# An attention layer on one core: GpSimd's scalings get fixed places, and the start makes half of the masks and heads

## The chip, the cores and the metric

The kernel runs on one NeuronCore of a Trainium2 chip. The metric is the time of one execution on the device in microseconds, in medians of several runs. The engines are named as in the profile: PE is TensorE (PEld its weight loads), DVE is VectorE, ACT is ScalarE, POOL is GpSimd and SP is SyncE, which here only issues transfers.

## The reference

The input x has 8 batches of 2048 rows and 256 channels, the adjacency matrix adj 2048 x 2048 integers, the same for all batches. With 8 heads of 32 channels the reference computes

```python
qkv = einsum('fnc,ck->fnk', x, w_qkv)            # q, k, v: (F, N, 8, 32)
scores = einsum('fnhd,fmhd->fhnm', q, k) / sqrt(32)
scores = where(adj > 0, scores, -1e9)
attn = softmax(scores, axis=-1)
t = einsum('fhnm,fmhd->fnhd', attn, v)           # back to (F, N, 256)
y = layernorm(x + t, ln1_g, ln1_b)
h = relu(y @ w1 + b1)
z = layernorm(y + h @ w2 + b2, ln2_g, ln2_b)
out = layernorm(x + z)
```

All of it is in float32.

## The kernel before

Only the path for these shapes (`fast_path`) runs. A batch is cut into 4 chunks of 512 query rows (`qc`), 2 groups of 4 heads (`g`) and 16 blocks of 128 key rows (`mb`, called a phase below). An item is one (batch, chunk, group, block). There are 8 x 4 x 2 x 16 = 1024 items, and the main loop takes one per step; 16 steps are a group, 128 steps a frame, which is one batch.

A step t does this: `exponentials(t+1)` on ACT (L237), `scores(t+2)` as 8 matmuls on PE (L230) with two additions of the mask on DVE (L233), `values(t)` as 8 matmuls on PE (L249), and `add_up(t)`. The last prepares the softmax denominators: blocks 3, 6, 8, 10, 12 and 14 are added on POOL to the tile of block 0 (L271), and blocks 4, 7, 11 and 5, 9, 13 are added by accumulating transfers, issued by POOL, to the tiles of blocks 1 and 2 (L268). Block 15 stays alone. `denominator` (L315) sums the four tiles that are left over the keys on PE. A tile of items, `p`, holds 1 MB; there are 12 of them in a ring, and each becomes free when the last reader of its old content is done: the sum or the transfer for most blocks, `denominator` for four.

Everything else is a filler. `advance(t)`, first in a step, resumes generators from a list sorted by due time. What PE does for a filler needs one PSUM bank, and credit (2200 a step, 1024 for a group of products) says how many are taken in a step, unless one is due. `yield 3` rests three steps, `yield BANK` asks for the bank. The fillers are `denominator`, `outcome` (the division by the denominators and the residual, fetched by an accumulating transfer), `tail`, and the next batch's rows (`turn`), projections (`project`) and queries (`ask`), which the table NEXT starts at fixed steps of a frame.

`tail` of a chunk is: `norm` (statistics on DVE L278 and L279, small operations on POOL, scaling on ACT L290), `feed_forward` with two products and on POOL a multiplication and an addition on 128 x 1024 (L459 and L461), a second `norm`, again a multiplication and an addition on POOL (L363 and L365), an accumulating transfer that adds x (L367), a third `norm`, and the output. On each engine, and on POOL's queue of transfers, instructions run in the order in which the program issues them.

`begin`, ahead of the loop, turns the rows of batch 0, projects both head groups, and makes the mask of all four chunks from adj: 16 loads of 1 MB, a conversion on DVE (L575), transposes on PE (L141), evacuation to fp8 on ACT (L147) or DVE (L145), and a store to a DRAM tensor MD. In the loop `load_mask` fetches each chunk's masks from MD.

Of the kernel before, what the change touches and what calls it, by code (L numbers as in the profile page):

```python
# [31 lines left out]

MASKED = -57344.0
CODE = -5.0
# [27 lines left out]
def fast_path(ctx, tc, cst, x, adj, out, RS):  # L62
# [7 lines left out]
    ld = ctx.enter_context(tc.tile_pool(name="ld", bufs=LD))  # L70
    kp = ctx.enter_context(tc.tile_pool(name="kp", bufs=3 * NCK - 1))
    qp = ctx.enter_context(tc.tile_pool(name="qp", bufs=4))
    vp = ctx.enter_context(tc.tile_pool(name="vp", bufs=3 * NCK - 1))
    pp = ctx.enter_context(tc.tile_pool(name="pp", bufs=12))
    work = ctx.enter_context(tc.tile_pool(name="work", bufs=1))
# [48 lines left out]
    MD = dp.tile([NCK, MB // 2, P, 2 * CH // 4], I32, name="md")  # L124
    MK = {}

# [6 lines left out]

    def mask_blocks(qc, mc, cv, to=None):
        for half in range(2):
            yield BANK
            ps = bank(BF16)
            for r in range(2):
                for j in range(TPC):
                    rr = 2 * half + r  # L140
                    nc.tensor.transpose(ps[:, r, j * P:(j + 1) * P], cv[:, j, rr * P:(rr + 1) * P], identb)  # L141
            k = 2 * mc + half
            m = to[half] if to else mask_piece(0, qc, k)
            if half:
                nc.vector.tensor_tensor(m, ps, cst["ones"][:, 0:1, None].to_broadcast([P, 2, CH]), ALU.min, saturate=False)  # L145
            else:
                nc.scalar.copy(m.bitcast(I8), ps)  # L147
            nc.sync.dma_start(MD[qc, k], words(m))

# [72 lines left out]
    def scores(item):  # L222
        f, qc, g, mb = item
        pt = PT[item] = pp.tile([P, 4, CH], F32, name="p")
        ps2 = [score_pair() for _ in range(2)]

        for half in (1, 0):
            for j in range(2):
                r = D * (2 * half + j)
                nc.tensor.matmul(ps2[half][:, j, :], KT[f, mb // TPC, g][r:r + D, (mb % TPC) * P:(mb % TPC + 1) * P],  # L230
                                 QT[f, qc, g][r:r + D, :], start=True, stop=True)
        for half, ps in enumerate(ps2):
            nc.vector.tensor_tensor(pt[:, 2 * half:2 * half + 2, :], ps,  # L233
                                    MK[f, qc, mb // 2][:, mb % 2, None, :].to_broadcast([P, 2, CH]), ALU.add)

# [36 lines left out]


    def norm(t, per=1):
        mv = small.tile([P, TPC, nc.vector.BN_AGGR_DIM], F32, name="mv")
# [11 lines left out]
        nc.gpsimd.tensor_scalar(nb, nb, -1.0, 1.0, op0=ALU.mult, op1=ALU.mult)  # L287
        yield 2
        for j in range(TPC):
# [7 lines left out]
    def denominator(f, qc, g, ready):  # L297
        grp = (f, qc, g)
        blocks = [ALONE, MOVED[0][0], POOLED[0], MOVED[1][0]]
        late = {2: ready - 1, 3: ready}  # L300
        if (f, qc, g) == items[-1][:3]:
# [31 lines left out]
    def outcome(f, qc):  # L333
        yield ROOM
        state["tails"] += 1
        xin = x[f, qc * CH:(qc + 1) * CH, :].rearrange("(p j) c -> p j c", p=P)
        y = yp.tile([P, TPC, C], F32, name="y")
        yield from divide(f, qc, y)
        nc.gpsimd.dma_start(y, xin, accum_op=ALU.add)
        begin = items.index((f, qc, 1, LAST)) + SUM + 2  # L340
        if (f, qc) == (F - 1, NCK - 2):
            start(begin + 5, tail(f, qc, y, xin, 2), begin + 8)
        else:
            start(begin + 10, tail(f, qc, y, xin), begin + 26)

# [10 lines left out]

    def tail(f, qc, y, xin, per=1):
        yield from norm(y, per)
        yield from feed_forward(y)
        yield 1  # L360
        z = y
        yield from norm(z, per)
        nc.gpsimd.tensor_tensor(z, z, rows(cst["g2r"]), ALU.mult)  # L363
        yield 1
        nc.gpsimd.tensor_tensor(z, z, rows(cst["be2r"]), ALU.add)  # L365
        yield 1
        nc.gpsimd.dma_start(z, xin, accum_op=ALU.add)  # L367
        yield 7
        yield from norm(z, per)
        nc.sync.dma_start(out[f, qc * CH:(qc + 1) * CH, :].rearrange("(p j) c -> p j c", p=P), z)  # L370
        state["tails"] -= 1
# [65 lines left out]
    def finish(f, qc):  # L437
        y = yp.tile([P, TPC, C], F32, name="y")
        xr, xb = state["rows"]
        yield from divide(f, qc, y)  # L440
        yT, hT = (work.tile([P, 2, CH], F32, name=n) for n in ("turned", "hT"))
        dst = out[f, qc * CH:(qc + 1) * CH, :].rearrange("(p j) c -> p j c", p=P)
        both = [half_rows(h, y, xr, xb, yT, hT, dst) for h in range(2)]
        while both:
            for e in list(both):
                if next(e, both) is both:
                    both.remove(e)

    def feed_forward(y):
        yield TURNED  # L450
        state["turned"] = True
        yT = work.tile([P, 2, CH], F32, name="turned")
        for a in range(2):
# [3 lines left out]
            nc.scalar.activation(yT[:, a, :], ps, AF.Identity, bias=cst["be1c"][:, a:a + 1], scale=cst["g1c"][:, a:a + 1])  # L457
        yield 1
        nc.gpsimd.tensor_tensor(y, y, rows(cst["g1r"]), ALU.mult)  # L459
        yield 1  # L460
        nc.gpsimd.tensor_tensor(y, y, rows(cst["be1b2r"]), ALU.add)  # L461
        hT = work.tile([P, 2, CH], F32, name="hT")
# [8 lines left out]
        state["turned"] = False  # L471
        yield 1
        z = y
# [62 lines left out]
    items = [(f, qc, g, mb) for f in range(F) for qc in range(NCK) for g in range(2) for mb in range(MB)]  # L536
    LEAD = 2
    FRAME = 2 * NCK * MB


    def ask(f, c):
# [4 lines left out]
    NEXT = {1: [(turn, 0)], 2: [(ask, 1)], 20: [(turn, 1)], 34: [(ask, 2)], 40: [(project, 0, 0)], 50: [(turn, 2)],  # L546
            60: [(project, 1, 0)], 66: [(ask, 3)], 72: [(turn, 3)], 80: [(project, 2, 0)], 98: [(ask, 0)], 100: [(project, 3, 0)],
            104: [(project, 0, 1)], 108: [(project, 1, 1)], 112: [(project, 2, 1)], 116: [(project, 3, 1)]}

    def begin():  # L550
        todo = deque((qc, c) for qc in range(NCK) for c in range(NCK))
        rows, cols = [], deque()

        def fetch():
            if todo:
                qc, c = todo.popleft()
                t = pp.tile([P, 4, CH], F32, name="p").bitcast(I32)
                nc.sync.dma_start(t, adj[qc * CH:(qc + 1) * CH, c * CH:(c + 1) * CH].rearrange("(j p) m -> p j m", p=P))
                cols.append((qc, c, t))

        for c in range(NCK):
            rows.append(pp.tile([P, 4, CH], F32, name="p"))
            xc = rows[c][:, 0:2, :].rearrange("p a (b c) -> p (a b) c", c=C)
            nc.sync.dma_start(xc, x[0, c * CH:(c + 1) * CH, :].rearrange("(j p) c -> p j c", p=P))
            fetch()
        fetch()
        while cols:
            qc, c, col = cols.popleft()
            if c % 2 == 0:
                two = pp.tile([P, 4, CH], F32, name="p").rearrange("p a q -> p (a q)").bitcast(BF16)  # L570
            cv = two[:, c % 2 * TPC * CH:(c % 2 + 1) * TPC * CH].rearrange("p (j m) -> p j m", m=CH)

            for half, what in enumerate((CODE, MASKED)):
                part = slice(half * 2 * P, (half + 1) * 2 * P)
                nc.vector.tensor_scalar(cv[:, :, part], col[:, :, part], 0.0, what, op0=ALU.is_le, op1=ALU.mult)  # L575
            fetch()
            xT = rows[c][:, 2:4, :]
            if qc == 0:
                yield from turn_rows(rows[c][:, 0:2, :].rearrange("p a (b c) -> p (a b) c", c=C), xT)
                nc.sync.dma_start(XD[0][c], xT)  # L580
                XT[0, c] = xT
                if c == 0:
                    yield from queries(0, 0, xT)
                yield from project(0, c, 0, xT)
            elif qc == 1:
                yield from project(0, c, 1, xT)
            if qc and c % 2 == 0:
                out4 = take([P, 4, 2, CH], F8)
                give(out4)
            yield from mask_blocks(qc, c, cv, [out4[:, c % 2 * 2 + i] for i in range(2)] if qc else None)  # L590
            if (qc, c) == (1, NCK - 1):
                for k in range(LEAD):
                    scores(items[k])
                exponentials(items[0])

    for _ in begin():
        pass
    state["side"] = 0
    for t, (f, qc, g, mb) in enumerate(items):
        if g == 1 and mb % 2 and (f + 1 < F or qc + 1 < NCK):  # L600
            load_mask(f + (qc + 1) // NCK, (qc + 1) % NCK, mb // 2)
        for what, *which in NEXT.get(t % FRAME, []):
# [268 lines left out]
```

## Time and profile before

| | us |
|---|---|
| median of the runs (3194.78 to 3200.07) | 3196.82 |
| the profiled execution | 3199.32 |
| its span | 3197.5 |
| first score matmul, PE L230 | 59.50 |
| first exponential of the loop (item 1) | 96.0 |
| starts of frames 1 to 7 | 466.7, 846.5, 1229.4, 1612.4, 1995.6, 2378.6, 2761.6 |
| last exponential | 3147.5 |

The span goes from the first to the last instruction of the profiled execution. A frame's start is the start of the exponential of its second item on ACT, the first that the frame's first step issues. The page gives for each group of instructions its busy time, the mean of one in ns, and the idle time of the engine ahead of it with what ended most of it. For a transfer it gives the time from issue to landing. Times in a timeline are from the start of the span.

### The profile page before, as it was taken

How to read it: one execution, taken by the hardware profiler on the slowest of the kernel's cores; microseconds unless marked ns; L12 is line 12 of the kernel's file. 1: busy time of each engine (PE TensorE's matmuls, PEld its weight loads, DVE VectorE, ACT ScalarE, POOL GpSimd, SP SyncE). 2: the span in 40 equal slices, each digit the busy share in tenths (PEclk: the TensorE clock that was granted, in tenths of full speed). 3: DMA queues.
4: the chain of work that ended last, by engine and by line, in shares of the span. 5: the costliest groups of instructions: out<-in, count | busy, mean ns of one | idle time of the engine just before them, and what ended most of it. 6: DMA issues, size and time to landing. Idle time of an engine off the chain costs nothing.

```text
span 3197.5 us, 68542 instructions
## 1 busy us (share of the span) xinstructions
PE 3098.8 (97%) x28996; PEld 980.3 (31%) x28996; DVE 2737.4 (86%) x3203; ACT 2438.4 (76%) x1941; POOL 2589.4 (81%) x1358
## 2 busy tenths in 40 slices
PE   7899999999999999999999999999999999999985
PEld 4222333233332333323333323323233233332222
DVE  4788888888889988888988988888888888889975
ACT  3677778778778777788777788778878778778764
POOL 0478888888888888789888889888888788879884
PEclk8899999999999999999999999999999999999998
DMA  9588889788879888789878889878889788878863
GB/s 322 141 193 189 181 180 194 178 190 193 182 175 210 186 191 175 175 193 208 190 172 176 190 185 221 174 169 199 180 193 207 170 191 196 178 170 167 178 142 71
DMA packets 153098, 589.49 MB, mean 184 GB/s; under 512 B 15024, under 2 KB 67760, under 8 KB 103888
## 3 DMA queue, kind: packets, MB, share of 16 engines
q0 software_dynamic: 64272, 433.75, 67.7%
q1 hardware_dynamic: 87696, 149.98, 13.4%
q8 instruction: 229, 3.75, 0.4%
q10 hardware_dynamic: 816, 1.31, 0.1%
q14 instruction: 85, 0.70, 0.1%
HBM read 146.67 MB, written 37.75 MB: 58 GB/s over the span
## 4 chain that ended last, share of the span: by engine, by line
PE 87%; DVE 5%; issue 2%; DMA 1%; POOL 1%; ACT 1%; DVEq 0%; ACTq 0%; POOLq 0%
PE s L230 32%; PE x L249 28%; PE x L54 16%; PE x L315 7%; DVE p L233 4%; PE x L95 4%; DMA p<-p 1%; DVE st L278 0%; POOL p L271 0%; DMA y<-in_x_dram 0%; DVE y L353 0%; ACT p L237 0%; PE s L54 0%; DVE mv L279 0%; ACT y L290 0%
## 5 line engine op out<-in xcount | busy, mean ns | idle before, releaser
L233 DVE TENSOR_TENSOR p<-s,mask 128x1024 f32<-128x1024 f32 x2048 | 2410.3, 1219 | 336.2 <-PE s L230 196.0
L237 ACT ACTIVATE p<-p 128x2048 f32<-128x2048 f32 x1024 | 1956.6, 1911 | 527.7 <-DVE p L233 453.7
L271 POOL TENSOR_TENSOR p<-p 128x2048 f32<-128x2048 f32 x382 | 1858.7, 4866 | 388.5 <-ACT p L237 388.2
L230 PE MATMUL s<-qT,kT 32*128 32x512 f32 x8192 | 1172.4, 642 | 40.9 <-DVE p L233 35.6
L249 PE MATMUL x<-p,v 128*32 128x512 f32 x8192 | 1092.7, 605 | 0.5 <-ACT oT L253 0.4
L230 PEld LDWEIGHTS s<-qT,kT 32*128 32x128 f32 x8192 | 320.8, 183 | 643.9 <-DVE p L233 602.5
L268 POOL DMA_DIRECT2D p<-p x382 | 408.1, 1070 | 78.4 <-ACT p L237 49.4
L249 PEld LDWEIGHTS x<-p,v 128*32 128x32 f32 x8192 | 161.4, 108 | 779.9 <-issue 289.8
L315 PE MATMUL x<-p,ones 128*32 128x512 f32 x2080 | 267.1, 592 | 0.6 <-DMA p<-p 0.5
L54 PE MATMUL x<-in,wqkv 128*32 128x512 f32 x1888 | 243.5, 592 | 0.0
L290 ACT ACTIVATE y<-y,nb,rs 128x256 f32<-128x256 f32 x372 | 218.4, 590 | 3.0 <-POOL nb L287 3.0
L278 DVE BATCH_NORM_STATS2 st<-y 128x6 f32<-128x256 f32 x372 | 155.1, 417 | 5.2 <-DMA y<-in_x_dram 5.2
L54 PE MATMUL x<-turned,w1s 128*32 128x512 f32 x992 | 122.5, 592 | 0.0
L54 PEld LDWEIGHTS x<-wqkv,in 128*32 128x32 f32 x3584 | 102.2, 110 | 63.5 <-issue 58.9
L54 PE MATMUL x<-w2s,hT 128*32 128x256 f32 x2016 | 121.1, 381 | 0.0
L54 PE MATMUL x<-wqkv,in 128*32 128x128 f32 x3584 | 117.3, 273 | 0.0
L315 PEld LDWEIGHTS x<-p,ones 128*32 128x32 f32 x2080 | 67.4, 110 | 156.8 <-issue 152.0
L54 PEld LDWEIGHTS x<-in,wqkv 128*32 128x32 f32 x1888 | 61.7, 110 | 140.9 <-issue 113.1
L284 POOL TENSOR_TENSOR rs<-rs,mhalf 128x4 f32<-128x4 f32 x93 | 96.2, 1035 | 7.7
L363 POOL TENSOR_TENSOR y<-y,g2r 128x1024 f32<-128x1024 f32 x31 | 99.3, 3205 | 1.9 <-ACT y L290 1.9
L365 POOL TENSOR_TENSOR y<-y,be2r 128x1024 f32<-128x1024 f32 x31 | 91.9, 2963 | 0.6
L54 PEld LDWEIGHTS x<-w2s,hT 128*32 128x32 f32 x2016 | 65.5, 111 | 70.5 <-issue 37.8
(116 smaller groups left out, 1342.1 us busy)
## 6 DMA issues: line engine op xcount, KB each, us to landing
p<-p POOLq DMA_DIRECT2D x382, 1024.0 KB, 9.7
in<-xd SPq DMA_DIRECT2D x87, 512.0 KB, 9.3
mask<-md SPq DMA_DIRECT2D x248, 128.0 KB, 7.9
y<-in_x_dram POOLq DMA_DIRECT2D x62, 512.0 KB, 9.5
p<-in_adj_dram SPq DMA_DIRECT2D x16, 1024.0 KB, 9.7
out_dram<-y SPq DMA_DIRECT2D x31, 512.0 KB, 5.9
in<-in_x_dram SPq DMA_DIRECT2D x29, 512.0 KB, 14.5
xd<-in SPq DMA_DIRECT2D x28, 512.0 KB, 10.7
```

Of the source, the lines that this page charges most:

```text
L54: nc.tensor.matmul(out[r:r + D], lhsT[:, r:r + D], rhs, start=start, stop=stop)
L95: nc.tensor.transpose(ps[:, j * P:(j + 1) * P], s, ident)
L230: nc.tensor.matmul(ps2[half][:, j, :], KT[f, mb // TPC, g][r:r + D, (mb % TPC) * P:(mb % TPC + 1) * P], QT[f, qc, g][r:r + D, :], start=Tr ...
L233: nc.vector.tensor_tensor(pt[:, 2 * half:2 * half + 2, :], ps, MK[f, qc, mb // 2][:, mb % 2, None, :].to_broadcast([P, 2, CH]), ALU.add)
L237: nc.scalar.activation(PT[item], PT[item], AF.Exp, scale=1.0 / math.sqrt(D))
L249: nc.tensor.matmul(O[grp][r:r + D, :], V[f, mb // TPC, g][:, mb % TPC, r:r + D], PT[item][:, h, :], start=(mb == 0), stop=(mb == LAST))
L268: nc.gpsimd.dma_start(PT[f, qc, g, chain[0]], PT.pop(item), accum_op=ALU.add)
L271: nc.gpsimd.tensor_tensor(first, first, PT.pop(item), ALU.add)
L278: nc.vector.bn_stats(st, t[:, j, :])
L290: nc.scalar.activation(t[:, j, :], t[:, j, :], AF.Identity, bias=nb[:, j:j + 1], scale=rs[:, j:j + 1])
L315: nc.tensor.matmul(ps[r:r + D, :], cst["ones"], term[:, h, :], start=(n == 0), stop=(n == len(blocks) - 1))
L363: nc.gpsimd.tensor_tensor(z, z, rows(cst["g2r"]), ALU.mult)
```

## The change

- `begin` makes the masks of chunks 0 and 1 only, from 8 loads, with all evacuations on ACT, and projects head group 0 only. `other_half` projects head group 1 of batch 0 as a filler in the first group.
- The masks of chunks 2 and 3 are made in the loop in 16 pieces, one `mask_job` begun every 5 steps from step 1. Each has one half of a tile of its own (`px`, which in later batches holds block 15).
- The ring of `p` tiles has 11 in place of 12, the pools of keys and values have one tile less.
- POOL's scaling operations wait for `calm()`: the phases 15, 0, 1, 2, 3, 4. The two closing ones (L363 and L365) are issued in one step. `tail` is split in `tail` and `closing`, with a due time of its own.
- `norm` rests `lag()` steps, from a table, where it rested 2. `denominator` reads its last block a step later.
- `load_mask` is issued 9 steps later; `project(2, 0)` and those after it move in NEXT.
- The last chunk but one starts its tail 3 steps later and adds preloaded rows on POOL in place of the accumulating transfer. `finish` gives the fillers a step in between.

```diff
-    kp = ctx.enter_context(tc.tile_pool(name="kp", bufs=3 * NCK - 1))
+    kp = ctx.enter_context(tc.tile_pool(name="kp", bufs=3 * NCK - 2))
...
-    pp = ctx.enter_context(tc.tile_pool(name="pp", bufs=12))
+    pp = ctx.enter_context(tc.tile_pool(name="pp", bufs=11))
+    px = ctx.enter_context(tc.tile_pool(name="px", bufs=1))
...
+    def mask_job(qc, k, h):
+        while h in used:
+            yield 1
+        used.add(h)
+        part = parts[h]
+        col = part.bitcast(I32).rearrange("p (j m) -> p j m", j=TPC)
+        nc.sync.dma_start(col, adj[qc * CH:(qc + 1) * CH, k * 2 * P:(k + 1) * 2 * P].rearrange("(j p) m -> p j m", p=P))
+        yield 5
+        cv = part.bitcast(BF16).rearrange("p (a b m) -> p a b m", a=2, b=4)[:, :, 0:2, :]
+        nc.scalar.copy(cv, part.bitcast(I32).rearrange("p (a b m) -> p a b m", a=2, b=2))
+        yield 1
+        yield BANK
+        ps = bank(BF16)
+        turn_mask(ps, [cv[:, j // 2, j % 2] for j in range(TPC)])
+        m = part[:, CH // 2:CH].bitcast(F8).rearrange("p (b q) -> p b q", b=2)
+        convert(m.bitcast(I8), ps)
+        yield 1
+        nc.sync.dma_start(MD[qc, k], words(m))
+        MADE.add((qc, k))
+        used.remove(h)
...
-        pt = PT[item] = pp.tile([P, 4, CH], F32, name="p")
+        pt = PT[item] = (px if f and mb == ALONE else pp).tile([P, 4, CH], F32, name="p")
...
+    CALM = (LAST, 0, 1, 2, 3, 4)
+
+    def calm():
+        return 1 + (LAST - 1 - state["now"]) % MB if (state["now"] + 1) % MB not in CALM else 1
+
+    def lag():
+        return (4, 4, 4, 4, 2, 2, 2, 2, 2, 2, 3, 3, 3, 4, 4, 4)[state["now"] % MB]
...
-        yield 2
+        yield lag()
...
-        late = {2: ready - 1, 3: ready}
+        late = {2: ready - 1, 3: ready + 1}
...
-            start(begin + 5, tail(f, qc, y, xin, 2), begin + 8)
+            xb = take([P, TPC, C], F32)
+            nc.sync.dma_start(xb, xin)
+            start(begin + 8, tail(f, qc, y, xin, begin + 11, 2, xb), begin + 11)
...
-            start(begin + 10, tail(f, qc, y, xin), begin + 26)
+            start(begin + 10, tail(f, qc, y, xin, begin + 33), begin + 27)
...
+    def closing(f, qc, y, second, xin, per, xb):
+        yield from second
+        yield 1
+        z = y
+        yield from norm(z, per)
+        if xb is None:
+            yield calm()
+            nc.gpsimd.tensor_tensor(z, z, rows(cst["g2r"]), ALU.mult)
+            nc.gpsimd.tensor_tensor(z, z, rows(cst["be2r"]), ALU.add)
+            yield 1
+            nc.gpsimd.dma_start(z, xin, accum_op=ALU.add)
+            yield 7
+        else:
+            nc.gpsimd.tensor_tensor(z, z, rows(cst["g2r"]), ALU.mult)
+            nc.gpsimd.tensor_tensor(z, z, xb, ALU.add)
+            yield 2
+        yield from norm(z, per if xb is None else TPC)
...
-        yield 1
-        nc.gpsimd.tensor_tensor(y, y, rows(cst["g1r"]), ALU.mult)
-        yield 1
-        nc.gpsimd.tensor_tensor(y, y, rows(cst["be1b2r"]), ALU.add)
+        scaled = []
+
+        def scale():
+            nc.gpsimd.tensor_tensor(y, y, rows(cst["g1r"]), ALU.mult)
+            nc.gpsimd.tensor_tensor(y, y, rows(cst["be1b2r"]), ALU.add)
+            scaled.append(state["now"])
+
+        def later():
+            yield calm()
+            scale()
...
+    def second_products(y, hT, scaled):
+        while not scaled or state["now"] < scaled[0] + 4:
+            yield 1
...
-            60: [(project, 1, 0)], 66: [(ask, 3)], 72: [(turn, 3)], 80: [(project, 2, 0)], 98: [(ask, 0)], 100: [(project, 3, 0)],
-            104: [(project, 0, 1)], 108: [(project, 1, 1)], 112: [(project, 2, 1)], 116: [(project, 3, 1)]}
+            60: [(project, 1, 0)], 66: [(ask, 3)], 72: [(turn, 3)], 98: [(ask, 0)], 100: [(project, 2, 0)],
+            104: [(project, 3, 0)], 108: [(project, 0, 1)], 112: [(project, 1, 1)], 116: [(project, 2, 1)], 120: [(project, 3, 1)]}
...
+        for c in range(NCK):
+            start(0, other_half(c, kept[c]), MB + TPC * c - LEAD - 1)
+
+    def other_half(c, xT):
+        if c == 0:
+            yield from channels(QT, qp, "qT", (0, 0, 1), xT, P)
+        yield from project(0, c, 1, xT)
...
+        uf, uqc, ug, umb = items[max(t - LATE, 0)]
+        if ug == 1 and umb % 2 and (uf + 1 < F or uqc + 1 < NCK):
...
+        if t % 5 == 1 and n_mask < (NCK - 2) * MB // 2:
+            mqc, mk = divmod(n_mask, MB // 2)
+            start(t, mask_job(2 + mqc, mk, n_mask % 2), t + 14)
+            n_mask += 1
```

## The prediction

> **What bounds the kernel now.** I read the page first: the busy shares, then the chain of waits, then the groups and transfers by name.
>
> ```profile
> span 3197.5 us, 68542 instructions
> PE 3098.8 (97%) x28996; PEld 980.3 (31%) x28996; DVE 2737.4 (86%) x3203; ACT 2438.4 (76%) x1941; POOL 2589.4 (81%) x1358
> PE 87%; DVE 5%; issue 2%; DMA 1%; POOL 1%; ACT 1%; DVEq 0%; ACTq 0%; POOLq 0%
> L233 DVE TENSOR_TENSOR p<-s,mask 128x1024 f32<-128x1024 f32 x2048 | 2410.3, 1219 | 336.2 <-PE s L230 196.0
> L271 POOL TENSOR_TENSOR p<-p 128x2048 f32<-128x2048 f32 x382 | 1858.7, 4866 | 388.5 <-ACT p L237 388.2
> p<-p POOLq DMA_DIRECT2D x382, 1024.0 KB, 9.7
> ```
>
> TensorE is busy 97% of the span and is 87% of the chain. By the spacing of the exponentials in the timeline, a step with one filler group on PE takes 2.925 us and a step without 2.49 us (2 mask adds of 1.22 on VectorE). From those I count a step as 2.07 us plus 0.86 us per filler group of four matmuls. A frame (one batch, 128 steps) then sums to 382.3 us, and 383.0 are measured between its first exponentials. So time is only won where PE stands still, and it stands still at the two ends. The table of windows shows the start (columns: span, then PE, PEld, DVE, ACT and POOL busy, PE clock, DMA share, GB/s):
>
> ```profile
> 60.00:100.00 40.00, 20.61 (x156) 14.20 (x152) 24.77 (x29) 11.82 (x10) 0.00 (x0) 0.53 0.49 167
> ```
>
> and the timeline of PE and VectorE shows the stall near the end:
>
> ```profile
> 3081.76 0.43 DVE L278 BATCH_NORM_STATS2 st<-y 128x6 f32<-128x256 f32 x1 [5.23 <-DMA y<-in_x_dram]
> 3084.20 2.09 PE L230 MATMUL s<-qT,kT 32*128 32x512 f32 x8 [6.61 <-DVE p L233]
> ```
>
> Between 60 and 100 us nothing but masks of quarters 2 and 3 is made; half the time PE waits for conversions, at a clock of 0.53. At 3081 a statistic at the head of VectorE's queue waits for the residual's transfer and holds up the mask adds, hence PE.
>
> Last, the timeline of GpSimd and VectorE at step 20 of the fourth frame, the place on which my forecast turns:
>
> ```profile
> 1285.74 4.59 POOL L271 TENSOR_TENSOR p<-p 128x2048 f32<-128x2048 f32 x1
> 1290.24 0.92 POOL L268 DMA_DIRECT2D p<-p  x1
> 1291.43 0.86 POOL L268 DMA_DIRECT2D p<-p  x1 [0.28 <-ACT p L237]
> 1294.20 4.57 POOL L271 TENSOR_TENSOR p<-p 128x2048 f32<-128x2048 f32 x1 [1.91 <-ACT p L237]
> 1299.34 2.36 DVE L233 TENSOR_TENSOR p<-s,mask 128x1024 f32<-128x1024 f32 x2 [0.86 <-ACT y L290]
> DMA to landing us min/median/max: 7.1/10.5/12.8
> ```
>
> The transfer issued at 1290.24 landed 7.1 us later, at 1297.3. It empties the tile that the mask adds at 1299.34 write: 2.0 us to spare. The one issued at 1291.43 landed at 1304.3, and the adds at 1305.87 write into its tile: 1.6 us to spare.
>
> **What the skill says.** "GPSIMD Engine Reference", section "3.1 Elementwise — side-by-side cycle accounting", gives 4497 ns for a GpSimd add of 2048 floats per partition; the trace agrees (4.57 alone, 4.87 mean). "DMA: Bandwidth & Descriptors", section "Issuing engines are not separate DMA queues", says transfers of all issuers run on the same 16 engines and interleave; the trace agrees: the same accumulate of 1 MB took 7.1 us first in its row and 12.8 behind another. Its section "SWDGE vs HWDGE vs iDMA" leaves accumulating transfers to GpSimd, so whatever stands ahead of them on GpSimd delays them; all 382 are on its queue here. "TensorE: Matmul & The Clock Gate", section "Part 1: The HAM clock gate (the \"warmup\" mystery)", puts an idle PE at half clock after a window of about 3.4 us; the 0.53 above agrees, and 16 mask transposes took 1.89 us in that stretch against 1.07 at full clock.
>
> **The change part by part**, against the profiled execution's 3199.3 us (span 3197.5; the median is 3196.8, 0.08% below).
>
> 1. *The beginning.* Before, the first score matmul is at 59.5 us, and the first exponential of the loop at 96.0. Now eight mask quarters, the second head group's projections and VectorE's half of the evacuations leave. Quarter 0 was done at 39.7; with all its evacuations on ACT, four more of 1.01 us, I take 44.3. Quarter 1's eight casts on ACT take 8 x 1.01, so ACT is free at 52.3 for the first exponential, PE's scores being ready before. Then two exponentials with their adds and scores at 1.9 to 4 us, start of the loop's first about 58.4. Gain 37.6.
>
> 2. *The same work in the loop.* Mask transposes of 16 pieces (0.54 us each on PE) and the second head group's products are fillers of frames 0 and 1. Steps that were empty take some of it for nothing: VectorE's 2.49 us hides the first 0.42 of PE's filler. By the instruction order the step sums are 363.4, 378.8, five of 382.3, 370.2 before, and 365.3, 390.9, five of 381.4, 370.7 after: in all 10.0 more. Cost 10. (Were no step empty it would be 14 more.) VectorE's own 1.2 us per piece is late against PE by up to 4.8 us in frame 0, where some 2.2 us are absorbed (my estimate: one item's two adds of 1.2 are ahead of PE's need by the lead of two): 5 with the 11 tiles that are left of 12.
>
> 3. *Mask pieces wait for their loads.* A copy on ACT stands 5 steps, 14.6 us, behind its 512 KB load. The nearest row, the input rows of the same size and width, landed in 14.5 us at the median, 5 to 6 in phases 0 and 1 of a group and 14.6 to 19 in phases 6 to 12. Seven of the 16 pieces begin in these; ACT would wait up to 4.4 us each, mean 2.2, with the exponentials behind it, and a few loads follow their store's landing (3.0 us). I take 18; bounds 5 (only the worst two late) and 40 (each of the seven at 4.4, the stores' waits on top). None can be a gain.
>
> 4. *GpSimd's scalings.* The first pair (L459, L461; 2.7 us each) moves to phases 15 or 1, where GpSimd has no sum to do: nothing; if its lag from the group before still stood there, 5 us would go to the denominator. The closing pair (L363, L365; 3.28 and 3.16 us at the median, 2.4 where VectorE is quiet) was one per step at phases 11 to 15 and 0. Now both stand at phase 4, ahead of the group's first accumulate transfer; then their own residual transfer (0.9), then the second accumulate. So the first is issued 4.8 to 6.4 later and lands at 1302 to 1303.7 where VectorE wants the tile at 1299.3: 2.8 to 4.4 late. The second is issued at about 1298, behind 512 KB more, and its tile is wanted one item sooner, at 1302.4 plus the first delay, for the tile's turn is now 3 steps where it was 4. It lands 7.1 to 12.8 us after its issue, 1305.1 to 1310.8, against 1305.2 to 1306.8: 0 to 5.6 more. Together 2.8 to 10, of which 2.2 is absorbed before PE stands. That leaves 0.6 to 7.8; since the second has two transfers ahead of it I take 5.5. Only the second group of a frame has so short a turn (3 steps); in the other three closings it is 5 and 6 steps, 5.8 us more, and nothing is late. Seven frames have this place: 7 x 5.5 = 38.5, ends 4 and 55. What is queued behind on GpSimd are the sums of steps 22 and 24 and so the denominators, which the lag of about 6 us leaves in time by one step, block 3 having been put a step later.
>
> 5. *Mask loads 9 steps later, project moves, the lag table.* They are issued on SP outside the path: masks land in 7.9 us and are wanted over 20 us later, 0. If SP stood behind a store, one step.
>
> 6. *The end.* The last chunk but one begins 3 steps later and adds its preloaded rows by GpSimd, 2.4 us in place of a transfer, so that the statistic finds its data: the stall of 8.6 us (6.6 and the half clock after) goes. What is late next is VectorE, 6.6 us behind at most in that frame against 4.9: perhaps 2. After the loop 1 is saved. Gain 8.6; ends 0 and 9.6.
>
> Sum: 3199.3 - 37.6 + 10 + 5 + 18 + 38.5 - 8.6 - 1 = 3224.
>
> **Rivals.** *(a) The tile turn does not stop PE.* For it: VectorE has idle gaps of 0.9 to 1.9 us around step 20, GpSimd stands 1.9 us before its next sum and so catches up, and a transfer alone lands in 6.9. Against: 2.0 us of slack against a pair of at least 4.8. It decides where the pair takes under about 4.2 us (2.0 + 2.2). Then 3224 - 38.5 = 3185, faster by 0.4%. With loads in time too, 3172. *(b) Transfers and mask loads both at their long ends*: the stalls at 55 and the ACT waits at 33 give 3185 + 55 + 15 = 3255. *(c) The start wins little*: ACT, with all evacuations and the weight of frame 0, becomes the bound until mask piece 16 is made (step 76), and PE falls to half clock between. For it, 16 copies of 1.0 us in 76 steps; against, ACT is busy 76%. At two such waits of 3.4 us and half clock as long after each, 10 to 20, it would cost 15 more: 3239. That the scalings would not really be both at phase 4 is no rival: the built order has them so in each of the steady frames.
>
> **How the numbers follow.** The stall at step 20 with the rest as summed: 0.52 (own range 3198 to 3248). Rival (a) 0.28, of it a little within 0.2%; (b) 0.12; (c) 0.08. The time is that of the first. The range of 8 in 10 goes from (a) with short waits to (b): 3174 to 3260. A measurement of this kernel can tell 0.2%, 6.4 us, from no change. Faster, below 3190.4: 0.26, from (a); same 0.08, (a) with long ACT waits or the stall at its low end; slower 0.66.
>
> **What would show it.** Step 1: first exponential of the loop near 58 and no idle stretch at 60 to 100. Step 3: ACT's copy waiting for its load, exponentials behind. Step 4: mask adds 5 and 6 items into the second group waiting for the accumulate transfer, PE idle 1 to 8 us there, frames 2 to 6 at 384 to 390 us rather than 383. Step 6: no VectorE wait on the residual near the end. The prediction is wrong if the frames stay at 382 (then rival (a)) or if frame 0 is much longer than 390.

## The result, and the profile after

The kernel became slower: 3480.44 us in the median of 4 runs (3471.92 to 3487.62) against 3197.4 for the kernel before, a ratio of 1.0884 (1.0858 to 1.091). The forecast was 3224, with a range of 3174 to 3260. The sign was right, the size was short by a factor of ten: a loss of 283 us in place of 27.

The page of the kernel after shows where to look (busy time and share of each engine, then the chain of waits by engine and by line, then three rows of groups and transfers):

```profile
span 3478.2 us, 68375 instructions
PE 3187.2 (92%) x28996; PEld 1000.8 (29%) x28996; DVE 2725.7 (78%) x3187; ACT 2451.5 (70%) x1957; POOL 2590.7 (74%) x1357
PE 42%; DMA 20%; DVE 16%; POOL 9%; ACT 2%; issue 2%; DVEq 0%; POOLq 0%; ACTq 0%; SPq 0%
PE s L248 16%; DMA p<-p 13%; DVE p L251 13%; PE x L267 13%; PE x L53 9%; DMA out_dram<-y 4%; POOL p L289 4%; PE x L341 3%; DMA mask<-md 3%; POOL y L398 2%; POOL y L397 2%; ACT p L255 2%; DVE st L304 1%; DVE y L381 1%; PE x L95 1%
L251 DVE TENSOR_TENSOR p<-s,mask 128x1024 f32<-128x1024 f32 x2048 | 2409.2, 1218 | 607.9 <-PE s L248 289.2
L289 POOL TENSOR_TENSOR p<-p 128x2048 f32<-128x2048 f32 x382 | 1830.3, 4791 | 254.1 <-ACT p L255 252.9
p<-p POOLq DMA_DIRECT2D x382, 1024.0 KB, 10.5
```

No engine but PE is busy longer by more than 1%: the mask adds (L251) and GpSimd's sums (L289) have the totals of before within 2%, and PE's same 28996 matmuls take 3187.2 us in place of 3098.8. The chain has changed its kind. PE was 87% of it and is 42%; transfers are 20%, led by the accumulates p<-p and by the stores of the output. The kernel is no longer bound by PE; half of its chain now runs through transfers, VectorE and GpSimd.

The start did what was forecast. The windows of the kernel after:

```profile
60.00:100.00 40.00, 39.82 (x412) 12.56 (x408) 32.69 (x29) 28.26 (x21) 26.22 (x10) 0.96 0.66 138
```

PE is busy in this stretch, and the first exponential of the loop is at 58.6 us (96.0 before). All of the loss lies in the frames. From one exponential to the one 128 steps later (frame 7 to the last exponential):

| frame | 0 | 1 | 2 | 3 | 4 | 5 | 6 | 7 |
|---|---|---|---|---|---|---|---|---|
| before | 370.7 | 379.8 | 383.0 | 383.0 | 383.2 | 383.0 | 383.0 | 385.9 |
| after | 419.0 | 435.1 | 423.0 | 417.8 | 422.4 | 419.3 | 418.1 | 413.8 |

Within frames 2 to 6 the 8 groups of 16 steps (groups 0 to 7; the second group of a frame is group 1) are longer by 10.1, 8.7, 0.0, 6.7, 2.5, 3.6, 2.2 and 3.2 us, 37.1 in all. The windows of group 0 and of the whole fourth frame, before and after, show what such a number holds:

```profile
1229.50:1277.50 48.00, 48.00 (x504) 16.27 (x500) 43.03 (x50) 35.67 (x27) 39.13 (x21) 1.00 0.73 152
1335.60:1394.00 58.40, 51.92 (x560) 19.00 (x556) 43.02 (x50) 36.52 (x29) 44.52 (x24) 0.94 0.75 165
sum 382.90, PE 381.73 PEld 119.50 DVE 336.73 ACT 302.18 POOL 324.25; mean PE 47.72 PEld 14.94 DVE 42.09 ACT 37.77 POOL 40.53
sum 417.80, PE 389.34 PEld 121.25 DVE 336.07 ACT 302.29 POOL 322.91; mean PE 48.67 PEld 15.16 DVE 42.01 ACT 37.79 POOL 40.36
```

Of the 10.4 us that group 0 grew here, PE stands idle for 6.5. The rest is PE's own work: the new tails move fillers into this group (560 matmuls, 504 before, fewer in later groups), and the clock is 0.94. So the length of one group is no pure measure of waiting.

Two places stand out in the timelines. The first is step 20, in GpSimd's timeline of the kernel after, fourth frame:

```profile
1402.12 4.57 POOL L289 TENSOR_TENSOR p<-p 128x2048 f32<-128x2048 f32 x1
1406.64 2.38 POOL L397 TENSOR_TENSOR y<-y,g2r 128x1024 f32<-128x1024 f32 x1
1409.10 2.39 POOL L398 TENSOR_TENSOR y<-y,be2r 128x1024 f32<-128x1024 f32 x1
1411.42 0.90 POOL L286 DMA_DIRECT2D p<-p  x1
1412.05 1.18 POOL L400 DMA_DIRECT2D y<-in_x_dram  x1
1412.61 1.51 POOL L286 DMA_DIRECT2D p<-p  x1
```

The sum of phase 3, the closing pair, the first accumulate, the residual, the second accumulate: the three transfers are issued within 1.2 us and land after 9.7, 10.9 and 15.4 us. VectorE's timeline shows who waits for them:

```profile
1421.29 2.35 DVE L251 TENSOR_TENSOR p<-s,mask 128x1024 f32<-128x1024 f32 x2 [6.98 <-DMA p<-p]
1428.09 2.36 DVE L251 TENSOR_TENSOR p<-s,mask 128x1024 f32<-128x1024 f32 x2 [4.17 <-DMA p<-p]
```

The mask adds of two items wait for the first and the second accumulate, 11 us together. GpSimd's largest new wait, for VectorE's statistics (201.6 us in total, 39.6 before), is not what delays them: in groups 1, 3, 5 and 7 the sum of block 3 starts 0.5 us after its exponential's end in both kernels, in the median of frames 2 to 6. The second place is one group earlier, where nothing was forecast (VectorE, GpSimd and SP):

```profile
1355.62 0.34 SPq L407 DMA_DIRECT2D out_dram<-y  x1
1367.35 0.69 DVE L381 TENSOR_TENSOR y<-x,rc 128x512 f32<-128x512 f32 x1 [4.54 <-DMA out_dram<-y]
1371.72 0.86 POOL L365 DMA_DIRECT2D y<-in_x_dram  x1 [6.20 <-DVE y L381]
```

A chunk's division by the denominators writes into one of two places for y. The old content of that place was sent to the output at 1355.62 and had left it at 1367.2, 11.6 us later. The division stands at the head of VectorE's queue until then, the mask adds behind it; GpSimd stands 6.2 us for the division, with a sum and an accumulate of p behind it.

### The profile page after: what moved, and what is told of

Read it like the earlier page. It is cut to its first block, busy times and chain, and to the rows that moved or that the text cites. A ratio compares the mean times of both kernels' runs of the same rounds, so it can differ in the third digit from the quotient of the medians.

```text
span 3478.2 us, 68375 instructions
## 1 busy us (share of the span) xinstructions
PE 3187.2 (92%) x28996; PEld 1000.8 (29%) x28996; DVE 2725.7 (78%) x3187; ACT 2451.5 (70%) x1957; POOL 2590.7 (74%) x1357
## 4 chain that ended last, share of the span: by engine, by line
PE 42%; DMA 20%; DVE 16%; POOL 9%; ACT 2%; issue 2%; DVEq 0%; POOLq 0%; ACTq 0%; SPq 0%
PE s L248 16%; DMA p<-p 13%; DVE p L251 13%; PE x L267 13%; PE x L53 9%; DMA out_dram<-y 4%; POOL p L289 4%; PE x L341 3%; DMA mask<-md 3%; POOL y L398 2%; POOL y L397 2%; ACT p L255 2%; DVE st L304 1%; DVE y L381 1%; PE x L95 1%
## 5 line engine op out<-in xcount | busy, mean ns | idle before, releaser
L251 DVE TENSOR_TENSOR p<-s,mask 128x1024 f32<-128x1024 f32 x2048 | 2409.2, 1218 | 607.9 <-PE s L248 289.2
L289 POOL TENSOR_TENSOR p<-p 128x2048 f32<-128x2048 f32 x382 | 1830.3, 4791 | 254.1 <-ACT p L255 252.9
L248 PE MATMUL s<-qT,kT 32*128 32x512 f32 x8192 | 1200.2, 656 | 184.1 <-DVE p L251 181.9
L267 PE MATMUL x<-p,v 128*32 128x512 f32 x8192 | 1117.5, 618 | 0.1
L286 POOL DMA_DIRECT2D p<-p x382 | 371.0, 981 | 232.7 <-DMA p<-p 140.1
L309 POOL TENSOR_SCALAR rs<-mv 128x4 f32<-128x4 f32 x93 | 17.8, 191 | 206.2 <-DVE mv L305 201.6
L53 PE MATMUL x<-wqkv,in 128*32 128x128 f32 x3584 | 127.9, 294 | 15.8 <-DVE y L381 15.1
L53 PE MATMUL x<-turned,w1s 128*32 128x512 f32 x992 | 133.2, 628 | 0.0
L53 PEld LDWEIGHTS x<-wqkv,in 128*32 128x32 f32 x3584 | 112.1, 119 | 70.9 <-issue 43.5
L365 POOL DMA_DIRECT2D y<-in_x_dram x31 | 27.1, 875 | 124.1 <-DVE y L381 118.7
## 6 DMA issues: line engine op xcount, KB each, us to landing
p<-p POOLq DMA_DIRECT2D x382, 1024.0 KB, 10.5
```

Of the source, the lines that this page charges most:

```text
L53: nc.tensor.matmul(out[r:r + D], lhsT[:, r:r + D], rhs, start=start, stop=stop)
L267: nc.tensor.matmul(O[grp][r:r + D, :], V[f, mb // TPC, g][:, mb % TPC, r:r + D], PT[item][:, h, :], start=(mb == 0), stop=(mb == LAST))
L286: nc.gpsimd.dma_start(PT[f, qc, g, chain[0]], PT.pop(item), accum_op=ALU.add)
L289: nc.gpsimd.tensor_tensor(first, first, PT.pop(item), ALU.add)
```

## The experiments

In these diffs minus lines are the kernel the run is built from, plus lines the experiment. All frames and waits named are of profiled executions, times are medians.

**Which part of the change.** The first two runs split it. One is the kernel after with all that concerns the tails set back. The diff shows the small edits; `closing`, `second_products`, `outcome` and `finish`, which are those of the kernel before again, are left out:

```diff
-        yield lag()
+        yield 2
...
-        late = {2: ready - 1, 3: ready + 1}
+        late = {2: ready - 1, 3: ready}
...
-            yield calm()
             nc.gpsimd.tensor_tensor(z, z, rows(cst["g2r"]), ALU.mult)
+            yield 1
             nc.gpsimd.tensor_tensor(z, z, rows(cst["be2r"]), ALU.add)
```

> The kernel after, with the tails, GpSimd's scalings, the rests of norm, the late reading of block 3 and the last chunks of the kernel before; start, mask pieces, tile ring and mask loads stay as after. Theory 1, the new tails carry the loss (closing pair at phase 4 and late stores of y): frames 2 to 6 fall from 420 to about 383 us, only the start's gain of 37 and about 45 lost in frame 0 to the mask pieces remain, 3205 us. Theory 2, the smaller ring and the moved masks carry it: it stays above 3400 us.

3217.91 us, ratio 1.0063 (1.0047 to 1.008). Its frames 2 to 6 last 382.8 to 385.8 us; the loss in the steady frames is gone. The other is the mirror image, the kernel before with only the tails of after:

> The kernel before, with the tails, scalings, rests of norm, late reading of block 3 and the last chunks of the kernel after; start, ring of 12 and mask loads stay as before. Theory 1: seven frames lose about 37 us each, 3450 us. Theory 2: within 20 us of before, 3200 us. If both parts are needed (the pair at phase 4 hurts only with 11 tiles), it lies between, about 3300 us.

3467.26 us, 1.0849 (1.0831 to 1.0867), frames 2 to 6 at 419.9 to 421.5. So the tails cost 262 us taken out of after (3480.4 - 3217.9) and 270 put into before. Start, mask pieces, ring of 11 and mask loads cost 21 together. Theory 2 is out as to the total. The smaller ring does decide where the loss falls: with 12 tiles the mask adds of group 1 still wait 12.5 us a frame for accumulates (10.5 in the kernel after), but those of groups 3, 5 and 7 only 2.0 together (11.6), while divisions wait 10.7 for stores (5.3).

**The closing pair spread again**, on the kernel after:

```diff
-            yield calm()
             nc.gpsimd.tensor_tensor(z, z, rows(cst["g2r"]), ALU.mult)
+            yield 1
             nc.gpsimd.tensor_tensor(z, z, rows(cst["be2r"]), ALU.add)
```

> The kernel after, with the closing pair issued as soon as its norm is done, one operation per step, as before; all else as after. If the pair at phase 4 is the cause of the tile waits in groups 1, 3, 5 and 7 (22 us a frame), seven frames win that: 3325 us, and less, down to 3230, if the tails then end earlier and the waits on the stores of y go as well. If the place of the pair does not matter: 3480 us.

3451.76 us, 29 gained, neither of the two answers. The trace shows why this does not separate the theories. The rests of norm end so late that the multiplication is issued at phase 1, where GpSimd stands 8.1 us a frame in the second group for ACT's scaling; the addition still falls to phase 4 ahead of the first accumulate, and the residual to phase 5 between the two. The wait that was to go only moved ahead.

**A third place for y**, `bufs=3` in place of 2 on the kernel after.

> The kernel after, with three places for y in place of two, so that a division never waits for the store of the chunk before last. If these waits carry the loss of groups 0, 2, 4 and 6 (15 us a frame): 3375 us, with groups 1, 3, 5, 7 unchanged. If that loss comes from GpSimd's queue alone: above 3460 us.

3432.5 us, 48 gained where 105 were expected. The division's waits for stores are gone from the trace, and group 0 falls from 10.1 to 5.7 us of loss. These waits are real, but half as dear as the table of groups suggested, which held moved work as well: in group 0 PE is idle 2.4 us a frame in this run and 5.5 in the kernel after.

**The rests alone**, `lag()` returning 2 on the kernel after.

> The kernel after with norm resting 2 steps everywhere, as before, in place of the table's 2 to 4. In the order of the program the closing pair then stands at phases 2 and 3, its residual transfer at 3 and 4, and the store of a chunk 4 or 5 steps ahead of the division that reuses its place, where after has them at 4, 5 and 1 step. Theory 1 (the rests push the chain of the tail onto phase 4 and onto the next division): the waits on stores go (15 us a frame) and most of the tile waits too: near 3270 us. If the fixed places alone do it, whatever the rests: above 3430 us.

3341.47 us, 139 gained where 210 were expected. In groups 1, 3, 5 and 7 the loss falls from 22.2 to 2.3 us a frame, which is about all of the gain: the pair, at phases 2 and 3 in the order of the program, runs ahead of the sum of block 3. The store of a chunk is 4 or 5 steps ahead of the division that needs its place, and no division waits for one. Yet groups 0, 2, 4 and 6 lose 15.4 us a frame together where they lost 14.9, 12.2 of it in group 0. Part of that is moved work again (640 matmuls in group 0 of the fourth frame), and part is a wait that the rests had kept away: ACT stands 9.2 us a frame for GpSimd's small operations of a norm, 0.0 in the kernel after.

The rests are not harmful in themselves. The same table, put alone into the run with the old tails:

> The run with the old tails (3217.9 us), with the table of rests in norm put back alone. In the program's order the closing pair stays at phases 13 to 15 and 0. Theory 1 (rests cost only by pushing what has fixed places onto phase 4 and onto the next division): within 5 us of 3218. If rests cost by themselves, as the gain of 139 us from taking them out of the kernel after could be read: 3300 us or more.

3229.99 us, 12 more than 3217.9 and not 80: a little over the 5 that were allowed, and a tenth of what taking them out had won. Rests cost most where a fixed place lies behind them.

**The pair at phase 4 alone**, put into the run with the old tails (with three places for y and room for three tails, so that no store is waited for):

```diff
+        while (state["now"] + 1) % MB != 4:
+            yield 1
+        yield 1
         nc.gpsimd.tensor_tensor(z, z, rows(cst["g2r"]), ALU.mult)
-        yield 1
         nc.gpsimd.tensor_tensor(z, z, rows(cst["be2r"]), ALU.add)
         yield 1
         nc.gpsimd.dma_start(z, xin, accum_op=ALU.add)
```

> The run with the old tails (3217.9 us), with one thing put back: the closing pair waits for phase 4 and both operations and then the transfer are issued there; with three places for y, so that no store is waited for. Theory 1: the tile waits of the second groups come back, 15 to 24 us a frame in seven frames: 3320 to 3390 us. If the pair at phase 4 is harmless by itself: 3220 us.

3379.0 us, 161 more. Groups 1, 3, 5 and 7 lose 8.1, 6.8, 5.0 and 1.5 us a frame, those of the kernel after lost 8.7, 6.7, 3.6 and 3.2; the groups between lose 0.6 at most. VectorE's timeline of this run, at step 20 of the fourth frame, has the wait of after:

```profile
1368.26 2.36 DVE L251 TENSOR_TENSOR p<-s,mask 128x1024 f32<-128x1024 f32 x2 [6.77 <-DMA p<-p]
```

This shows the pair with its transfer at phase 4 as a cause by itself. It reaches groups 3, 5 and 7 too, where the forecast gave the tiles 5 and 6 steps. The table of waits (us in total, times, the longest):

```profile
DVE p L251 <- DMA p<-p: 149.1, 40, 6.8
POOL p L286 <- DMA p<-p: 79.1, 36, 5.0
```

An accumulate into a tile waits for the one before into the same tile. In group 3 the second accumulate landed 22.2 us after the end of its exponential in the median of frames 2 to 6 (12.2 in the kernel before), and VectorE waited at phase 11, 4.9 us a frame, to write into the tile that this accumulate empties. GpSimd waited 4.4 us a frame for the same landing, with the next accumulate of the chain at its head.

**Pair or transfer.** In that run the residual transfer alone is moved from phase 5 to 15 (`yield 1` becomes `yield 11`).

> The run with the old tails and the pair at phase 4 (3379.0 us), with the closing's residual transfer issued at phase 15 in place of phase 5. If the two operations ahead of the accumulate are the cost: above 3340 us. If it is mostly the third transfer flying between the two accumulates: below 3280 us. My guess is 3310.

3319.87 us, between the two theories and near the guess: of the 161, 59 went with the transfer. The other 102 are not all the two operations. Against the kernel before, groups 1, 3, 5 and 7 lose 8.8 us a frame here and lost 21.4 (in a profiled execution 10 us above the median), so most of the tile waits went with the transfer; but groups 0, 2, 4 and 6 now lose 6.6 where they lost 0.9. The move puts the third norm and the store 10 steps later too, and what that costs was not run by itself. In group 1 the second accumulate landed after 12.5 us where it took 15.0 with the residual ahead.

**The pair elsewhere.** The kernel after with a third y, and the pair waiting for phases 15, 0, 1 or 2:

```diff
-            yield calm()
+            while (state["now"] + 1) % MB not in (LAST, 0, 1, 2):
+                yield 1
+            yield 1
...
-                elif e[2] == TURNED and state["turned"] or e[2] == ROOM and state["tails"] == 2:
+                elif e[2] == TURNED and state["turned"] or e[2] == ROOM and state["tails"] == 3:
```

> The kernel after with three places for y and room for three tails, and the closing pair waiting for phases 15, 0, 1 or 2: in the program's order it stands at 15 and its residual transfer at 0. Theory 1: against the run with a third y (3432.5 us), the tile waits of groups 1, 3, 5 and 7 go, 24 us a frame, so about 3265 us. If something else in the new tails makes the tiles late (rests, late reading of block 3, statistics in front of GpSimd's sums): above 3400 us.

3315.25 us, 117 gained where 168 were expected. Groups 1, 3, 5 and 7 lose -2.2 us together instead of 23.7, as foreseen. But groups 0, 2, 4 and 6 now lose 7.9, 2.3, 3.3 and 3.3. A possible cause is VectorE: with the pair 11 steps later the third norm's statistics fall into phases 7 to 10, beside the second norm's statistics, the reciprocal and the two divisions. By the order of the program VectorE has 1.3, 1.7, 1.9 and 1.9 us there beside 2.4 of mask adds, in steps of 2.9 us. Two runs move those statistics, by the rest after the residual transfer: 4 in place of 7,

> The run with a third y and the closing pair at phase 15 (3315.3 us), with the third norm beginning 4 steps after its residual transfer in place of 7. Its statistics then leave phases 8 to 11, where VectorE also has the two divisions and the reciprocal. Theory 3, what is left in groups 0, 2, 4 and 6 (17 us a frame) is VectorE with more than a step's time of work in phases 8 to 11: about half goes, 3260 us. If what is left comes from GpSimd waiting for the division: 3315 us.

3341.12 us, slower where a gain was expected. The waits (frames 2 to 6) show another one in its place: in groups 0, 4 and 6 a statistic waits 2.2 to 2.9 us a frame for the residual, which had not landed after 4 steps. The other way, 11 in place of 7:

> The run with a third y and the pair at phase 15 (3315.3 us), with the third norm beginning 11 steps after its residual transfer in place of 7: its statistics then stand at phases 11 to 14, where VectorE has nothing but mask adds. Theory 3, the rest of that run's loss is VectorE's work in phases 7 to 10 (1.3 to 1.9 us beside 2.4 of mask adds in a step of 2.9; 10 us a frame over what is absorbed): 3245 us. If the division's wait on GpSimd's queue or the rests carry it: 3315 us.

3306.27 us, where 3245 was expected: 9 gained, with runs that just overlap (3301.05 to 3312.08 here, 3310.10 to 3316.72 there). Groups 0, 2, 4 and 6 fall from 16.8 to 9.2 us, but groups 1, 3, 5 and 7 rise from -2.2 to 1.9, frame 0 is 21 us longer, and frame 5 has 400 us where its neighbours have 392. So bunched work on VectorE is at most a part of that run's rest, and the remainder was not settled.

**The late reading of block 3** put back on the kernel after (`3: ready`).

> The kernel after with the last block of the denominator read a step sooner, as before. If the late reading holds tiles that the ring of 11 needs: 3440 us or less. If the tiles that are late are those of the transfers alone: 3480 us.

3479.64 us: no effect. That the tile of block 3 stays a step longer costs nothing, as the forecast had it.

**What the other parts cost.** The run with the old tails starts at 58.5 us in place of 96.0, but its frames 0 and 1 last 411.0 and 392.4 (370.7 and 379.8 before): 37.5 gained, 53 lost. Its table of waits has two transfers that before did not:

```profile
ACT p L156 <- DMA p<-in_adj_dram: 15.2, 3, 8.0
DVE p L251 <- DMA mask<-md: 12.9, 2, 11.9
```

The mask loads at their steps of before (`LATE = 0`):

> The run with the old tails (3217.9 us), with the mask loads issued at their steps of before, 9 steps sooner. Theory: the 12 us in which VectorE waits for a mask at step 62 go, 3205 us; frame 0 becomes 399 us from 411. If the masks' making is what is late, not the load's place: 3218 us.

3205.48 us, 1.0023 (1.0015 to 1.0031); frame 0 is 400.0. That is just the 12 us. Next, a half of the mask tile kept until its store has landed, so that a load is issued when the program counts it (`LATE` is 3 here):

```diff
         MADE.add((qc, k))
+        yield 3
         used.remove(h)
```

> The run with the old tails (3217.9 us), with mask loads issued 6 steps sooner than after has them and a half of the mask tile kept 3 steps longer after its store is issued, so that the next load does not stand on SP behind the store's landing and ACT's copy comes 5 steps after a load that is really issued. Theory: the 12 us of a mask's wait at step 62 and the 18 to 20 us of ACT waiting for adj loads go, about 3190 us. If only the first: 3205 us.

3194.88 us, 0.9987 (0.998 to 0.9994); frame 0 is 385.0 and ACT's waits for adj are gone. The last part is the end. Preloaded rows and a later tail for the last chunk but one, as after has them, with the bias added:

> The run before with masks mended, and the last chunk but one as in the kernel after: tail 3 steps later and preloaded rows (with the bias added on GpSimd) in place of the accumulating transfer. Theory: the stall of 8.6 us near the end goes, 8 us below the run with masks mended, about 3182 us, which would beat the kernel before by 15 us. If the later tail only moves the end: the same as with masks mended.

3199.54 us, no gain: the 6.2 us at the residual are gone, but PE stands 7.2 us for an exponential at phase 1 of the last group, with ACT waiting 8.2 for GpSimd's small operations of that norm, and what follows the loop takes 5 us longer. With four steps' rest in that norm, and the finish and the undivided last norm of after:

> The run with masks and end mended (3199.5 us), with 4 steps' rest in the first norm of the last chunk but one, the finish of the kernel after, and its last norm in one go, so that ACT does not stand 7 us on GpSimd at the start of the last group. Theory: the 8.6 us near the end are then really won, 3187 us. If the end is bound by the chain of that chunk's last norm: 3197 us.

3190.32 us, 0.9972 (0.9964 to 0.9981): 0.3% faster than the kernel before, and 4.6 us below the run with masks mended. Frame 7 is 378.9 us (385.9 before), what follows the last exponential 52.2 (50.0). Here the change's start and end are kept, its fixed places are not. The page of this run is back to

```profile
PE 3094.7 (97%) x28996; PEld 976.3 (31%) x28996; DVE 2725.0 (85%) x3187; ACT 2453.5 (77%) x1957; POOL 2591.2 (81%) x1358
```

## Why the prediction was wrong

The step that failed is term 4, what moving GpSimd's scalings costs. It was put at 38.5 us, and the pair with its transfer at phase 4 alone cost 161. Beside it stood a term that was left at nothing without a reason: the whole tail moves later, and with it the store that frees a place for y.

*The beginning (1)* came out: forecast 58.4 for the first exponential of the loop, measured 58.6; the gain is 37.4, forecast 37.6. That it agrees to 0.2 us is luck, since runs with the same start have 56.7 to 60.5. ACT was free as forecast (its last cast ends at 51.4, forecast 52.3), but PE's scores were not "ready before": the first exponential of all waited 3.7 us for the mask adds and stands at 55.2.

*The same work in the loop and the loads (2 and 3)* were 33 us in the sum. The run with the old tails loses 53 in the two frames. ACT's waits for adj measured 15.2, forecast 18, and mending them won 10.6; their cause was the one named last there, a load behind its store's landing. The wait for a mask, 12.4, was not in the sum at all. With both mended 25 us are still lost in the two frames, where term 2 had 15.

*Mask loads (5)* were put at nothing, "wanted over 20 us later". A mask wait of 11.9 us in frame 0 of the run with the old tails shows that the cover was not there: with 9 steps less, the load of a chunk's first mask is issued 4 steps before its use. SP had stood behind a store and then issued seven transfers within 8 us, and the load landed 20.2 us after its issue. The text's price for that case was "one step", and the wait is about four of them. The steps of cover could have been counted in the order of the program.

*GpSimd's scalings (4)*, on which the forecast turned, had the right place, mechanism and queue, and failed in three ways.

First, the size. The second group of a frame lost 8.7 us for a forecast of 5.5. The pair took 2.38 and 2.39, so the delay was at its low end; but with three transfers in flight the two accumulates landed after 9.7 and 15.4 us (8.2 and 14.5 in the median), where 7.1 and 7.1 to 12.8 were put. The sentence of the Trainium skill that transfers interleave ("DMA: Bandwidth & Descriptors", section "Issuing engines are not separate DMA queues") was cited and then not applied to the first of the three. The trace of before gave no warning of it: there the first of two took 7.1 us, and 6.9 to 7.1 is the median of all groups.

Second, of the other three closings the text says that "nothing is late": they lost 13.5 us a frame. There the second accumulate landed 16.1 to 17.0 us after its issue, and the mask adds of item 13 waited for its tile, 3.4 to 4.4 us a frame. So the cover of 5 and 6 steps was measured against a landing that was put too early, and with a ring of 12, where these adds come one item later, little of that wait is left.

Third, a stall of PE was priced by its length. In the windows by group of the fourth frame the granted clock of the groups with stalls is 0.94, 0.94 and 0.97, where it was 1.00; PE's busy time in that frame is 389.3 us in place of 381.7. Of the frame's 34.9 us, 27.3 are idle PE and 7.6 are longer work, which goes with the lower clock. The forecast had counted that for the stall at the end only. (The half clock that it shows between 60 and 100 us is no example of a long idle stretch: no gap of PE there is over 3.1 us.)

*The step that was missing* is the place for y. The change moves the closing of a tail by 5 to 8 steps, and the store of a chunk from 7 to 11 steps ahead of the division that reuses its place to one step ahead of it in the order of the program. The text looked at who waits for the pair. The rests (the lag table) stand in term 5 at 0, with a reason that speaks of mask loads only. What is late next was the chunk after the next, which cost 48 us by the run with a third y. The rests turned out to be what pushes the pair onto phase 4 and the store onto the division. Without the rests 139 us are won, about all by the pair's place: the store's waits go too, but other waits and moved work take their room.

*The end (6)*: the 8.6 us were not won. In the seventh group of the last frame PE still waits 4.6 us at one place (6.6 before), with VectorE 3.4 us at the residual (5.2 before). The text took the wrong transfer for the cause. The one that is waited for in both traces is the residual of the division, issued at L339 before and at L365 after; the preloaded rows replace another, that of the closing. So only the 3 steps could help, and in the kernel after this transfer landed 11.2 us after its issue (9.6 before). After the loop 1.2 us were lost where 1 was to be saved (51.2, 50.0 before). The run b3 shows that 7.0 can be won in the last frame, once ACT does not wait for GpSimd.

*The rivals*: (a), that the tile turn does not stop PE, is refuted by the pair put alone into the old tails. (b) had the right direction with ends far too near, 55 for the stalls where the new tails cost 262 to 270. (c) is not what happened: the start was won, and ACT is busy 264.7 of the 370 us from 100 to 470.

What stays open: the parts that were measured alone, 161 for the pair at phase 4 and 48 for the place for y, make 209 of the 262 to 270 us; the runs do not say where the others come from, nor that the parts add. Of the 97 us that the kernel after with a third y and the pair at 15 still loses (3315.3 - 3217.9), bunched work on VectorE may be a part, and the rest is not known. The same holds for groups 0, 2, 4 and 6 of the run without rests. That the division could wait for a store in the run with the pair at phase 4 and two places for y was not tried.

## What to carry to other kernels

When a stage is moved in a chain of fillers, follow every buffer it holds to its next user, not only the queue it is put on: here the output's place, two chunks on, cost more than the largest loss in the forecast (48 us, 38.5). An operation on the engine that issues accumulating transfers can be paid twice, by its own time and by the transfers that it lets start together; and the next accumulate into the same tile stands in the queue until the last has landed. Fixed places for work are only as good as the phase at which the work becomes ready, so count the steps up to it before choosing them. And a group that grows has not waited for all of it: look at the engine's work in it first.

## What was not expected of the hardware

Accumulates of 1 MB in the median of frames 2 to 6: the one at phase 4 of the second group landed 7.0 us after its issue in the kernel before and 8.2 in the kernel after, the one at phase 5 12.7 and 14.5, and 17.0 in group 3 of the kernel after (12.0 before). The residual of 512 KB between the two is paid mostly by the transfer behind it: in groups 3, 5 and 7 of the run with the pair at phase 4 the first landed after 8.0 to 8.1 us and the second after 14.3 to 17.0; with the residual moved away it was 6.9 to 7.0 and 11.2 to 14.3. And the two operations of the closing pair took 2.38 and 2.39 us at phase 4, where the same operations had medians of 3.28 and 3.16 at their old places. Why is not shown: VectorE was busy with mask adds at both.
